# Sums of the exponentials in window attention: one product of 294 columns over both halves of a unit in place of two of 147

## The chip, the cores and the metric

The kernel runs on one core of a Trainium2 chip. The core has five engines that run side by side: TensorE (PE, with its weight loads shown apart as PEld), VectorE (DVE), ScalarE (ACT), GpSimd (POOL) and SyncE (SP, which here only starts transfers). The metric is the time of one execution on the device in microseconds (us); smaller is better. Everything is computed in 32-bit floating point.

## The reference

The input is 16 images of 56 x 56 tokens with 384 channels. Layer 0 normalizes each image over 32 groups of channels, rolls it, cuts it into 7 x 7 windows and runs attention with 12 heads of 32 channels inside each window, with a relative position bias and, at two borders, a mask. Layer 1 normalizes again and applies a 3 x 3 depthwise convolution with binary weights. Both are added to their input.

```
qkv = x @ w_qkv.T
score = einsum('bhwqd,bhwkd->bhwqk', q, k) / sqrt(32) + rel      # per window: 49 x 49
attn = softmax(score)                                            # exp, divided by its sum over the keys
out = einsum('bhwqk,bhwkd->bhwqd', attn, v) @ w_out.T + b_out
x = x + roll(out)
x = x + depthwise3x3(group_norm(x), sign(w))
```

The change concerns the sum over the keys in the softmax.

## The kernel before, in words

**Strips and units.** An image is cut into eight strips of seven rows (`NS` = 8), a strip has eight windows and is worked on in two units of four windows each (`UPS` = 2, `UW` = 4). There are 256 units in all; the even unit is the first of its strip, the odd one the second. In a strip of 392 tokens all large products have 392 columns: `query_key` (L472, tiles pq), `value` (L485, pv) and `project` (L656, py), each with three blocks of 128 input channels for each of its output tiles.

**The order.** Nothing is scheduled by a program at run time: `all_units` writes the instructions in the order in which every engine then takes them. `heavy(u)` lists the large products of a unit in six steps. An even unit has `value` of the next strip in steps 0 to 2 and half of `query_key` of the next strip in steps 3 to 5; an odd unit has the other half of `query_key` in steps 0 to 2 and `project` of its own strip in steps 3 to 5. After step 0 come, for the unit itself, `add_up`, `invert`, `attend` and `divide`. The `scores` and the `softmax` of the next unit follow step 2 in an even unit and step 3 in an odd one (`then`), and its `exponential` one step later. The normalization and the convolution of the image before lie between, as a list of due times (`plan_load`, `plan_conv`); the convolution's taps (L784) are DVE's largest work.

**A unit's attention.** A unit has two halves `r` of two windows `w` each. `scores` (L526) multiplies keys by queries with the array cut into tiles of 32 rows by 64 columns and puts the scores into the tile ps: four banks, one for each head `i` of a group of four, with the three groups `j` and the two halves `r` side by side (294 columns). The keys of window `w` lie on partitions 64w to 64w+48. `softmax` (L543) scales, adds the bias and writes the tile e in SBUF in the order (i, j, r, query); `exponential` (L561, ACT) replaces it by its exponential. `add_up` (L597) then sums over the keys with a matrix of ones: the array is cut into tiles of 64 rows by 32 columns, so eight tiles (four `i`, two `w`) can work side by side. Each product in 32 bits is two passes, and each pass is a weight load and a matmul instruction. The sums go into the columns 294 to 440 of ps's four banks, bank 2r+w. `attend` (L617) multiplies e by v, 48 products of 49 columns, into the two banks po, in the order j, r, i, w. The values v (two buffers) were put in place by `by_key` (L508), 16 transfers issued by SP during the even unit before; the first products of `attend` in an even unit wait for them.

**What follows the sums.** `invert` takes the logarithm (L635) and its negative exponential (L636) on ACT, and one step of refinement on DVE (L637, L638). The tiles ln and inv have 588 columns for each partition. L637 is the last to read ps, which has one buffer, so the `scores` of the next unit wait for it. `attend`'s result is copied out of po by ACT (L627), and `divide` (L645, DVE) multiplies it by the inverted sums; `project` waits for that.

**Banks.** Four further PSUM banks serve pq, pv, py and po in turn. So pv's second tile in an even unit takes the bank of the last py of the strip before, which DVE reads in L664 (the addition of y).

Of the kernel before, what the change touches and what calls it, by code (L numbers as in the profile page):

```python
# [9 lines left out]
F32 = mybir.dt.float32  # L10
I32 = mybir.dt.int32
AF = mybir.ActivationFunctionType
ALU = mybir.AluOpType
# [21 lines left out]
def kernel(  # L35
# [12 lines left out]
    nc = tc.nc  # L48
    P = 128
    B, H, W, C = x.shape  # L50
    NH = rel_table.shape[1]
    D = C // NH
    NC = C // P
    HPC = P // D
    T = WIN * WIN
# [3 lines left out]
    UW = 4  # L59
    UPS = NW // UW  # L60
    NU = NS * UPS
    HT = 64
# [21 lines left out]
    ptpool = ctx.enter_context(tc.tile_pool(name="pt", bufs=3))  # L84
# [14 lines left out]
    ones = const.tile([P, P], F32, tag="ones", name="ones")  # L99
# [20 lines left out]
    es = const.tile([P, NH, 2, HT], F32, tag="e", name="e")  # L120
# [334 lines left out]
    vs, ots, pts, ys = {}, {}, {}, {}  # L455
    raw, sums = {}, {}
# [127 lines left out]
    def by_head(u):  # L584

        flat = es.rearrange("k h w q -> k (h w q)")[:, : NH * 2 * T]
        return flat.rearrange("k (h r q) -> k h r q", h=NH, r=2)

    def add_up(u):

        e = by_head(u)
        su = raw[u][:, :, NC * 2 * T : NC * 3 * T]
        for r in range(2):
            for i in range(HPC):
                for w in range(2):
                    keys = slice(w * HT, w * HT + T)
                    nc.tensor.matmul(  # L597
                        su[i * D : (i + 1) * D, 2 * r + w].rearrange("p (j q) -> p j q", j=NC),
                        ones[keys, :D],
                        e[keys, i * NC : (i + 1) * NC, r],  # L600
                        start=True,
                        stop=True,
                    )
        sums[u] = su

    def attend(u, fast):
# [24 lines left out]
    def invert(u):  # L631

        su = sums[u]
        ln, inv = (ptpool.tile([P, UW, NC * T], F32, tag="pt", name=f"{name}_{u}") for name in ("ln", "inv"))
        nc.scalar.activation(ln, su, AF.Ln, bias=least)  # L635
        nc.scalar.activation(inv, ln, AF.Exp, scale=-1.0, accum_out=reach[:, 1, u : u + 1])  # L636
        nc.vector.scalar_tensor_tensor(ln, su, -1.0, inv, ALU.mult, ALU.mult)  # L637
        nc.vector.scalar_tensor_tensor(ln, ln, 2.0, inv, ALU.add, ALU.mult)  # L638
        sums[u] = ln

    def divide(u):

        s, n = divmod(u, UPS)
        ot = ots[s][:, :, n * UW * T : (n + 1) * UW * T].rearrange("p j (w q) -> p j w q", w=UW)
        nc.vector.tensor_tensor(ot, ot, sums.pop(u).rearrange("p w (j q) -> p j w q", j=NC), ALU.mult)  # L645

    def project(s, m):

# [322 lines left out]
    def all_units(fast):  # L971
# [13 lines left out]
        for u in range(B * NU):  # L985
            todo = heavy(u)
            light = [(w, f, a) for w, f, a in sorted(side.pop(u, []), key=lambda i: i[0])]
            more = u + 1 < B * NU

            then = NC if u % UPS else NC - 1  # L990
            for i in range(len(todo)):
                run(todo[i])
                if i == 0:
                    if fast:
                        add_up(u)
                    else:
                        for j in range(NC):
                            transpose(u, j)
                    if fast:
                        invert(u)  # L1000
                    attend(u, fast)
                    if fast:
                        divide(u)
                if i == then and more:
                    scores(u + 1, fast)
                    softmax(u + 1, fast)
                if i == then + 1 and more:
                    exponential(u + 1, fast)
                while light and light[0][0] - u <= (i + 1) / len(todo):
                    _, g, a = light.pop(0)  # L1010
                    g(*a)
            for _, g, a in light:
                g(*a)
# [112 lines left out]
```

## Time and profile before

| what | value |
|---|---|
| median of three runs | 4131.12 us (4129.32 to 4135.01) |
| span of the profiled execution | 4128.7 us |
| granted TensorE clock, mean | 0.991 |
| DVE: taps L784, 752 instructions | 1378.4 us busy, 1833 ns each |
| DVE: L637, L638, L645, 256 each | 765, 771, 771 ns each |
| ACT: L635, L636, L561, 256 each | 752, 693, 1185 ns each |
| PE: products of 392 columns, L472, L485, L656 | 1587.5, 814.5 and 816.1 us busy |
| PE: scores L526, 24576 instructions | 340.7 us busy, 225 ns each |

The span is that of the one execution that the profiler recorded, from its first to its last instruction; the median is of separate runs and is 2.4 us longer. "Busy" of PE is the union of the intervals in which at least one matmul ran; matmuls overlap, and their ends are modelled, so a group's busy time is smaller than its count times its mean. "Idle before" is the time that an engine stood still just ahead of the group, with what ended it. A timeline merges neighbours of one group; its columns are start, length, engine, line, operation, tiles, shape and count.

### The profile page before, as it was taken

Reading aid. Unit: us, or ns where it says so; the run is one execution under the profiler, and the core shown is the slowest. Engines: PE = TensorE matmul, PEld = TensorE weight load, DVE = VectorE, ACT = ScalarE, POOL = GpSimd, SP = SyncE. Lnnn points to the kernel's source line nnn. Section 1 sums busy time; section 2 is a strip of 40 time slices with the busy share of each in tenths; the row PEclk is TensorE's granted clock in tenths of the full one; section 3 lists DMA queues with packets and bytes.
Section 4 is the critical chain, followed back from the end, with each engine's and each line's share of the span. In section 5 each row is a group of like instructions: output and inputs, shape, how many; then the busy total and the mean of one; then the engine's idle time right before and its main releaser. Section 6 shows DMA issues by size and latency. Waiting matters only on the chain.

```text
span 4128.7 us, 153178 instructions
## 1 busy us (share of the span) xinstructions
PE 4041.2 (98%) x67257; PEld 2554.0 (62%) x67257; DVE 3495.7 (85%) x3711; ACT 2237.9 (54%) x4654; POOL 1875.3 (45%) x3165
## 2 busy tenths in 40 slices
PE   5999999999999999999999999999999999999997
PEld 3666666666666666666666666666666666666656
DVE  4555989889898998989889898988989889898897
ACT  2545646555565655655555564655556555564552
POOL 5444435545453554445445453554545455452000
PEclk8999999999999999999999999999999999999998
DMA  4434556555665665556555555665556565554544
GB/s 94 79 60 90 110 100 126 105 109 103 116 114 108 116 113 103 110 98 127 106 115 108 109 116 103 117 115 100 114 100 121 104 122 109 101 121 77 107 100 109
DMA packets 1524022, 439.45 MB, mean 106 GB/s; under 512 B 1458970, under 2 KB 1473979, under 8 KB 1523346
## 3 DMA queue, kind: packets, MB, share of 16 engines
q1 hardware_dynamic: 1432680, 267.66, 38.1%
q0 software_dynamic: 87648, 159.12, 15.7%
q8 instruction: 531, 8.70, 0.9%
q10 hardware_dynamic: 3018, 2.78, 0.3%
q14 instruction: 145, 1.19, 0.1%
HBM read 169.63 MB, written 158.46 MB: 79 GB/s over the span
## 4 chain that ended last, share of the span: by engine, by line
PE 68%; issue 10%; DVE 9%; POOL 7%; DMA 4%; ACT 1%; SPq 1%; DVEq 0%; ACTq 0%; POOLq 0%
PE pq L472 28%; PE pv L485 14%; PE py L656 13%; PE ps L526 6%; PE po L617 5%; POOL xl L419 5%; DVE o L784 4%; PE ps L597 3%; DMA xl<-in_x_dram 1%; DMA mvd<-mv 1%; DVE e L543 1%; SPq L508 1%; POOL dev L268 1%; DVE st L452 1%; DVE y L664 1%
## 5 line engine op out<-in xcount | busy, mean ns | idle before, releaser
L472 PE MATMUL pq<-xn,wq_t 128*128 128x392 f32 x4608 | 1587.5, 497 | 0.1
L419 POOL DMA_DIRECT2D xl<-in_x_dram x1980 | 1331.2, 722 | 162.1 <-DVE xt L436 99.6
L784 DVE SCALAR_TENSOR_TENSOR o<-hp,dw_t,o 128x1568 f32<-128x1568 f32 x752 | 1378.4, 1833 | 5.4
L472 PEld LDWEIGHTS pq<-xn,wq_t 128*128 128x128 f32 x4608 | 846.6, 188 | 596.5 <-issue 1.9
L485 PE MATMUL pv<-xn,wq_t 128*128 128x392 f32 x2304 | 814.5, 497 | 4.7 <-DVE y L664 3.5
L656 PE MATMUL py<-ot,wo_t 128*128 128x392 f32 x2304 | 816.1, 499 | 3.0 <-DVE ot L645 3.0
L479 ACT COPY qk<-pq 128x392 f32<-128x392 f32 x768 | 369.9, 483 | 661.1 <-PE pq L472 660.1
L676 POOL COPY y<-y 128x63 f32<-128x63 f32 x128 | 54.5, 426 | 1314.6 <-DVE y L664 1314.6
L656 PEld LDWEIGHTS py<-ot,wo_t 128*128 128x128 f32 x2304 | 427.4, 190 | 298.0 <-DVE ot L645 6.9
L485 PEld LDWEIGHTS pv<-xn,wq_t 128*128 128x128 f32 x2304 | 423.6, 188 | 304.1 <-DVE y L664 5.3
L561 ACT ACTIVATE e<-e 128x1176 f32<-128x1176 f32 x256 | 303.2, 1185 | 417.9 <-DVE e L543 416.9
L637 DVE SCALAR_TENSOR_TENSOR ln<-ps,inv 128x588 f32<-128x588 f32 x256 | 195.9, 765 | 386.0 <-ACT inv L636 381.2
L492 ACT COPY vt<-pv 128x392 f32<-128x392 f32 x384 | 189.3, 493 | 431.6 <-PE pv L485 430.9
L526 PEld LDWEIGHTS ps<-qk 32*64 32x64 f32 x24576 | 308.5, 131 | 144.3 <-issue 123.0
L617 PE MATMUL po<-e,v 49*32 49x49 f32 x24576 | 368.9, 212 | 8.8 <-DMA v<-vq 7.9
L617 PEld LDWEIGHTS po<-e,v 49*32 49x32 f32 x24576 | 357.9, 105 | 16.4 <-issue 8.8
L543 DVE SCALAR_TENSOR_TENSOR e<-ps,bias 128x1176 f32<-128x1176 f32 x256 | 347.3, 1357 | 14.2 <-PE ps L526 13.9
L526 PE MATMUL ps<-qk 32*64 32x49 f32 x24576 | 340.7, 225 | 1.7 <-DVE ln L637 1.6
L448 ACT COPY x<-xt 128x196 f32<-128x196 f32 x720 | 225.6, 368 | 173.8 <-DVE xt L436 173.6
L496 DVE STREAM_TRANSPOSE vq<-vt 128x512 f32<-128x512 f32 x384 | 265.8, 693 | 8.9 <-ACT vt L492 5.4
L664 DVE TENSOR_TENSOR y<-py,x 128x392 f32<-128x392 f32 x384 | 213.2, 555 | 51.2 <-PE py L656 47.9
L461 ACT ACTIVATE xn<-x,coef 128x392 f32<-128x392 f32 x384 | 247.1, 711 | 14.5 <-DMA coef<-cod 14.5
(173 smaller groups left out, 3349.6 us busy)
## 6 DMA issues: line engine op xcount, KB each, us to landing
v<-vq SPq DMA_DIRECT2D x2048, 48.0 KB
xb<-mid SPq DMA_DIRECT2D x90, 855.5 KB
out_dram<-o SPq DMA_DIRECT2D x736, 98.0 KB
mid<-y POOLq DMA_DIRECT2D x112, 619.5 KB
xl<-in_x_dram POOLq DMA_DIRECT2D x1260, 52.5 KB
mid<-y POOLq DMA_DIRECT2D x15, 354.0 KB
xl<-in_x_dram POOLq DMA_DIRECT2D x180, 28.0 KB
mid<-y POOLq DMA_DIRECT2D x15, 265.5 KB
```

The lines of the kernel that those rows point to most:

```text
L419: nc.gpsimd.dma_start(xz[i * D + lo : i * D + hi, c, k : k + n, :], flat[token : token + n * (hi - lo)].rearrange("(k t) c -> t k c", k=n) ...
L472: nc.tensor.matmul(pq[:, :ST].rearrange("p (w t) -> p w t", t=T), wq_t[:, c, m * P : (m + 1) * P], xn[:, c, :, :T], start=(c == 0), stop=( ...
L479: nc.scalar.copy(qk[:, m, :ST], pq[:, :ST])
L485: nc.tensor.matmul(pv[:, :ST].rearrange("p (w t) -> p w t", t=T), wq_t[:, c, 2 * C + m * P : 2 * C + (m + 1) * P], xn[:, c, :, :T], start= ...
L496: nc.vector.transpose(vq[:, :, :, m].rearrange("p h n d -> p n h d"), vt[:, m].rearrange("p (n w) (j b) -> p n (w j) b", w=2, b=D),)
L526: nc.tensor.matmul(pp[row * HT : (row + 1) * HT, i, k0 : k0 + T], qk[part, NC * fast + j, q0 : q0 + HT], qk[part, NC * (not fast) + j, q0 ...
L543: nc.vector.scalar_tensor_tensor(e, pp[:, :, : NC * 2 * T].rearrange("q i (n k) -> q i n k", k=T), QSCALE, bias[:, int(s % NS == NS - 1)]. ...
L561: nc.scalar.activation(flat, flat, AF.Exp, accum_out=reach[:, 0, u : u + 1])
L617: nc.tensor.matmul(po[w][i * D : (i + 1) * D, (2 * j + r) * T : (2 * j + r + 1) * T], vs[s][keys, n * 2 + r, h * D : (h + 1) * D], by_head ...
L656: nc.tensor.matmul(py[:, :ST], wo_t[:, c, m * P : (m + 1) * P], ots[s][:, c, :], start=(c == 0), stop=(c == NC - 1),)
L664: nc.vector.tensor_tensor(view.rearrange("p r (w c) -> p w r c", c=WIN), py[:, :ST].rearrange("p (w r c) -> p w r c", r=WIN, c=WIN), xs[s] ...
L784: nc.vector.scalar_tensor_tensor(acc, by_half(hp[:, dy : dy + BR, dx : dx + W]), dw_t[:, c, t : t + 1], acc, ALU.mult, ALU.add)
```

## The change

`add_up` gives the array both halves `r` at once. In the tile e the three groups `j` and the two halves `r` of a head `i` are contiguous, 3 x 2 x 49 = 294 elements, so one product for each `i` and `w` has 294 columns where there were two, one for each `r`, of 147. The result goes into the first 294 columns of the first two banks of ps, where the scores of heads `i` = 0 and 1 were, and no longer beside the scores of all four banks. The tiles ln and inv keep their 588 columns, now as 2 x 294, and `divide` reads them in the new order. All else is unchanged.

```diff
     def add_up(u):
 
-        e = by_head(u)
-        su = raw[u][:, :, NC * 2 * T : NC * 3 * T]
-        for r in range(2):
-            for i in range(HPC):
-                for w in range(2):
-                    keys = slice(w * HT, w * HT + T)
-                    nc.tensor.matmul(
-                        su[i * D : (i + 1) * D, 2 * r + w].rearrange("p (j q) -> p j q", j=NC),
-                        ones[keys, :D],
-                        e[keys, i * NC : (i + 1) * NC, r],
-                        start=True,
-                        stop=True,
-                    )
+        flat = es.rearrange("k h w q -> k (h w q)")[:, : NH * 2 * T]
+        su = raw[u][:, 0:2, : NC * 2 * T]
+        for i in range(HPC):
+            for w in range(2):
+                keys = slice(w * HT, w * HT + T)
+                nc.tensor.matmul(
+                    su[i * D : (i + 1) * D, w],
+                    ones[keys, :D],
+                    flat[keys, i * NC * 2 * T : (i + 1) * NC * 2 * T],
+                    start=True,
+                    stop=True,
+                )
         sums[u] = su
...
     def invert(u):
 
         su = sums[u]
-        ln, inv = (ptpool.tile([P, UW, NC * T], F32, tag="pt", name=f"{name}_{u}") for name in ("ln", "inv"))
+        ln, inv = (ptpool.tile([P, 2, NC * 2 * T], F32, tag="pt", name=f"{name}_{u}") for name in ("ln", "inv"))
...
     def divide(u):
 
         s, n = divmod(u, UPS)
-        ot = ots[s][:, :, n * UW * T : (n + 1) * UW * T].rearrange("p j (w q) -> p j w q", w=UW)
-        nc.vector.tensor_tensor(ot, ot, sums.pop(u).rearrange("p w (j q) -> p j w q", j=NC), ALU.mult)
+        ot = ots[s][:, :, n * UW * T : (n + 1) * UW * T].rearrange("p j (r w q) -> p j r w q", r=2, w=2)
+        nc.vector.tensor_tensor(ot, ot, sums.pop(u).rearrange("p w (j r q) -> p j r w q", j=NC, r=2), ALU.mult)
```

## The prediction

> **What bounds the kernel now.** I read the page's busy shares first, then the groups by line, then the timeline of PE over two strips, then the instructions of the two lines concerned in one unit of each kind.
>
> ```profile
> PE 4041.2 (98%) x67257; PEld 2554.0 (62%) x67257; DVE 3495.7 (85%) x3711; ACT 2237.9 (54%) x4654; POOL 1875.3 (45%) x3165
> ...
> L617 PE MATMUL po<-e,v 49*32 49x49 f32 x24576 | 368.9, 212 | 8.8 <-DMA v<-vq 7.9
> ...
> L597 PE MATMUL ps<-e,ones 49*32 49x147 f32 x8192 | 188.8, 291 | 6.6 <-ACT e L561 6.5
> ```
>
> PE is busy in 98% of the span, and in 3886 of the 3896 us from 124 to 4020 us (the view by windows). So an interval removed from PE's stream is time, unless another engine is late behind it. The changed line has 188.8 us; its neighbour L617, which follows it in every unit, 368.9 us.
>
> ```profile
> 1993.22 0.74 PE L597 MATMUL ps<-e,ones 49*32 49x147 f32 x32
> 1993.75 1.23 PE L617 MATMUL po<-e,v 49*32 49x49 f32 x96
> ...
> 2008.39 0.73 PE L597 MATMUL ps<-e,ones 49*32 49x147 f32 x32
> 2008.93 1.66 PE L617 MATMUL po<-e,v 49*32 49x49 f32 x96
> ...
> 2024.01 0.73 PE L597 MATMUL ps<-e,ones 49*32 49x147 f32 x32
> 2024.54 1.28 PE L617 MATMUL po<-e,v 49*32 49x49 f32 x96
> ...
> 2039.24 0.73 PE L597 MATMUL ps<-e,ones 49*32 49x147 f32 x32
> 2039.77 1.27 PE L617 MATMUL po<-e,v 49*32 49x49 f32 x96
> ```
>
> The columns are start, length, engine, line. The same 96 instructions of `attend` take 1.66 us in the unit at 2008 and 1.23 to 1.28 us in others. Over the whole trace they take 1.284 us on average in the odd units (the second of a strip) and 1.594 us in the even ones, the first unit left out. What differs is seen in the instructions of L617 inside the long one:
>
> ```profile
> L617 PEld LDWEIGHTS po<-e,v x15: 102/103/105, 2008.8 to 2009.6; 49*32 49x32 f32 x15
> L617 PE MATMUL po<-e,v x14: 200/201/202, 2008.9 to 2009.5; 49*32 49x49 f32 x14
> L617 PEldq EVENT_SEMAPHORE  x6: 51/51/51, 2008.9 to 2009.5; - x6
> ...
> L617 PEldq EVENT_SEMAPHORE  x2: 51/51/51, 2008.5 to 2008.6; - x2
> ```
>
> Between 2008.8 and 2009.6 only 14 of 96 products start, between event-semaphore instructions; two more of these stand earlier, during the sums. There are 949 of them on L617 in the trace: eight in most even units (they wait for the sixteen DMAs of `by_key`, landed long before), five in the units of the kind at 2039.77, none in odd ones.
>
> **What the Trainium skill says.** "TensorE: Matmul & The Clock Gate", the table at its head: TensorE's queue is 64 instructions deep, a partial reorder window that pulls weight loads ahead of running matmuls. The trace agrees. The 32 products of one unit's sums are, with their loads, 64 instructions. In an odd unit (starts in ns after the first sum) the sums start in four waves of eight, at 0-47, 153-200, 278-326 and 404-453. The loads of `attend` start at 406, 466, 483, 500 and so on to 583, then nothing to 720. The first sum ends at 310, its second pass at 153+283=435, the second pass of the first product of the second half at 404+283=687; the stops end 31 to 33 ns after the last two (466, 720). So an instruction enters as one leaves, in program order. "Perfetto Trace Analysis", Identifying Dependency Chains: a wait on several engines may get event-semaphore instructions put ahead. They are the 949 above; in the trace an event semaphore and the waiting load behind it repeat every 125 ns. "PSUM — Partial Sum Buffer", The four PSUM rules: one output fits one bank, 512 fp32 columns; 294 do. No run here shows that limit.
>
> **The change part by part.** Built, the two programs have the same instructions and waits in the same order on all five engines, but for the sums: 16 products of 147 columns become 8 of 294, each issued as two passes, so 32 load and product pairs become 16. The wait of the first one (for the exponential) stays.
>
> (a) The streaming. Waves of 147 columns are 126 ns apart, products of 392 columns 329 ns: 0.829 ns a column and 4 ns each, so 248 ns for 294. The second wave starts 27 ns late today (153 instead of 126); kept, the new ones start at 0 and 126+27-126+248=275, and `attend` can start at 523 against 531 now. 8 ns by 256 units is 2.0 us. Nearly all columns stream as before, so this is all that the product itself gives.
>
> (b) The room in the queue. With 32 instructions for the sums instead of 64, 32 of `attend` (16 pairs, the first half of its first `j`) can enter before the first sum starts, and all its event semaphores stand among those 16 pairs. They need 8 by 125 ns, 1.0 us. It is there: the exponential that the sequencer passes first ends 2.7 us (median) before an even unit's sums, at the least 0.98 us in the full stretch, and the last pv products (329 ns a pass) run meanwhile. In the even units the chain of waits, now from 460 to 1161 ns after the first sum, should be gone, and `attend` takes what it takes in an odd unit. Price: 1.594-1.284=0.310 us by 127 units=39.4 us. The five-semaphore units (1.27 us) already have no loss and are in the mean.
>
> (c) Odd units gain nothing more: the queue holds 16 pairs of `attend` when it stops at 583 now; after, 16 or 17 when it stops until the second pass of the first sum ends, 275+406+33=714 against 720.
>
> (d) Who is late next. Where pv waits for the addition of y, an earlier end of `attend` is only a longer wait:
>
> ```profile
> PE pv L485 <- DVE y L664: 3.5, 13, 0.4
> ...
> PEld pv L485 <- DVE y L664: 5.3, 13, 0.6
> ```
>
> This is one even unit of an image's eight, 15 of 127 (13 named here); their 0.35 us each are lost: -5.3 us. In the other even units pv comes 0.6 us or more after the addition, so 0.37 us less leaves it uncovered nowhere. The next scores come 1.1 us or more after L637 has read the sums. L656 after L645 stands in odd units, whose timing stays. DVE is the fullest: 29.88 of 30.80 us in one strip's window, 0.9 us left for 0.37. Cover is thin there; I take no loss and keep 10 us of it for the range.
>
> (e) Reading the sums. L635 and L637 read two banks by 294 instead of four by 147: 588 elements either way (752 and 765 ns), at nothing. L645 reads them in runs of 49 as before; heads and halves merge into one step, so it stays a three-step pattern. 771 ns; at most 0.15 us more, beside other PE work. The read scores are used up before the exponential, so writing on them adds no wait.
>
> Sum: -39.4+5.3-2.0=-36.1 us. The span 4128.7 gives 4092.6; the median of the runs, 4131.1, is 2.4 us above the profiled span, so 4095. I take 4096, with a microsecond for DVE.
>
> **The rivals.** The uncertainty of this measurement is about 0.2%, 8.3 us; I call less no change.
>
> A, only the streaming: the sequencer doesn't pass `attend`'s waits while sums stand unfinished, so they come when they come now. For it: the first two stand at 111-141 and 236-266 ns in the even units, never before the sums. Against: by then the queue is full, which explains it too, and in the scores a load that waits (the 30th or so) goes through with the first burst. It gives 4131-2=4129; up to 4125.
>
> B, DVE takes the place: the fullest strips (four of eight) give back what they gain, 12 to 25 us, because taps delay the division and the additions. For it: the 0.9 us above, and py after L645 by 0.1 us in one odd unit of eight. Against: DVE still waits 0.2 to 2 us for L636 in most units. It gives 4108 to 4120, say 4113.
>
> C, slower: the queue's room isn't counted in instructions but is tied to the sums as a group, so that `attend` enters only as sums leave. Longer passes leave later: the first pair at 310+123+33=466 instead of 343, the next at 714 instead of 466. Every unit would then lose 0.25 us, 63 us in all: 4194. An eighth of it is past the bound. It decides if fewer than two pairs of `attend` enter before the first sum ends. For it: no `attend` load starts before 406 now. Against: 33 pairs get in before the first stop both for sums (147 columns) and for scores (49 columns), so it counts instructions.
>
> D, that the change doesn't do what it says: the built order shows that it does.
>
> **How the numbers follow.** Forecast 0.70, own range 4084 to 4108: below by the odd units' best (1.18 us instead of 1.28, 12 us), above by the DVE term. B 0.11, A 0.09, C and any other loss 0.10. The range that leaves out no more than 0.2 reaches from 4082 to 4124: it takes in B and the edge of A. Faster by over 0.2% is the forecast and B, 0.81; within, A, 0.09; slower 0.10.
>
> **What would show it.** L597 with 4096 products of 294 columns, about 405 ns each and 186 us busy: (a). L617's busy time near 256 by 1.28, that is 328 to 335 us with the union of overlaps, from 368.9; even units at 1.2 to 1.3 us; its event semaphores before the sums' start: (b). Odd units within 0.03 us of now: (c). More waiting of pv for L664 in that one unit of eight, and no new waits of PE on DVE: (d). L635, L637 and L645 at 752, 765 and 771 ns: (e). Event semaphores still between the products of `attend` would make it A; odd units at 1.5 us, C.

## The result, and the profile after

The changed kernel takes 4110.36 us (median of four runs, 4108.16 to 4112.23); the kernel before, run beside it, 4131.23 us (4129.32 to 4135.01). The ratio is 0.9949, with an interval from 0.9935 to 0.9963: 20.9 us faster, where 35 were forecast. The profiled execution has a span of 4108.1 us at a clock of 0.991, as before.

The page of the changed kernel (all lines behind the edit have moved up by one, so L617 is now L616):

```profile
span 4108.1 us, 144986 instructions
...
PE 4017.7 (98%) x63161; PEld 2490.6 (61%) x63161; DVE 3496.3 (85%) x3711; ACT 2236.7 (54%) x4654; POOL 1873.2 (46%) x3165
...
L616 PE MATMUL po<-e,v 49*32 49x49 f32 x24576 | 345.5, 212 | 10.3 <-DMA v<-vq 9.6
```

PE has 4096 products fewer and is busy 23.5 us less (4041.2 before); nearly all of it is `attend`, 345.5 us after 368.9. DVE's busy time is the same. The groups by line show the sums and what reads them:

```profile
L636 DVE SCALAR_TENSOR_TENSOR ln<-ps,inv 128x588 f32<-128x588 f32 x256 | 196.1, 766 | 368.5 <-ACT inv L635 367.9 <-PE po L616 0.4
...
L596 PE MATMUL ps<-e,ones 49*32 49x294 f32 x4096 | 186.3, 421 | 6.5 <-ACT e L561 6.4
```

The sums lost 2.5 us of busy time (188.8 before). Their readers cost what they did (766 ns here; 753 for L634 and 771 for L644). The timeline of PE over an even and an odd unit:

```profile
1999.23 0.73 PE L596 MATMUL ps<-e,ones 49*32 49x294 f32 x16
1999.75 1.45 PE L616 MATMUL po<-e,v 49*32 49x49 f32 x96
...
2014.62 0.73 PE L596 MATMUL ps<-e,ones 49*32 49x294 f32 x16
2015.14 1.29 PE L616 MATMUL po<-e,v 49*32 49x49 f32 x96
```

The unit at 1999 is one with eight event semaphores. Its `attend` takes 1.45 us where such units took 1.66, but the forecast was 1.2 to 1.3. An event semaphore is here an instruction of its own, ahead of a load that has several semaphores to wait for; in this trace the load names one of them and the event semaphore the rest. The instructions of L616 in the 0.92 us from the first sum on (count, shortest, median and longest duration in ns, first and last start):

```profile
L616 PEld LDWEIGHTS po<-e,v x14: 103/104/107, 1999.5 to 2000.1; 49*32 49x32 f32 x14
L616 PE MATMUL po<-e,v x13: 200/203/203, 1999.8 to 2000.1; 49*32 49x49 f32 x13
L616 PEldq EVENT_SEMAPHORE  x8: 51/51/51, 1999.3 to 2000.1; - x8
```

All eight are still there, and none stands before the first sum: the same line has no instruction from 1995 to 1999.23. That is the prediction's step (b), which had put all eight ahead of the sums, seen to fail in one row.

Over all units, from the first sum to the first large product behind `attend`, which is the stretch that the change can reach (ns, means of 127 units of each kind, read from the starts in the trace):

| | before | after | difference |
|---|---|---|---|
| even units | 2102 | 1976 | -126, 16.0 us in all |
| odd units | 1743 | 1702 | -41, 5.2 us in all |
| `attend` alone, even / odd | 1594 / 1284 | 1450 / 1256 | -144 / -28 |
| first event semaphore after the first sum, median | 105 | 21 | -84 |

The two differences make 21.2 us: the whole gain lies here, and what was lost and won elsewhere cancels. The mean of the even units hides a spread. Their median falls by 185 ns (from 2105 to 1920), but the units where pv waits for y gain nothing, and in a few others v landed later than before.

Where the gain comes from shows in one even unit, the same in both traces (ns after its first sum). Before, the event semaphores of `attend` start at 141 and 266; then comes a stop until 460, and then one starts every 125 ns to 1085, with the last waiting load at 1161. After, they start at 21, 146, 271 and so on every 125 ns to 896, with no stop, and the last waiting load at 972. The chain of waits is the same, but it begins 120 ns earlier in this unit (84 at the median) and has no stop at the full queue, 69 ns more: 189 ns less at its end. Forecast was that all of it would lie before the first sum.

What the chain costs can be read inside the changed kernel's trace, since not all even units have eight event semaphores. The median stretch is 1591 ns in the 16 units with five, 1650 in the 13 with six and 1930 in the 96 with eight (1730, 1845 and 2117 before). So from six to eight each one adds about 140 ns (136 before), and five cost less than their number would make them: they lie in part behind the sums.

### The profile page after: what moved, and what is told of

Read it like the earlier page. It is cut to its first block, busy times and chain, and to the rows that moved or that the text cites. A ratio compares the mean times of both kernels' runs of the same rounds, so it can differ in the third digit from the quotient of the medians.

```text
span 4108.1 us, 144986 instructions
## 1 busy us (share of the span) xinstructions
PE 4017.7 (98%) x63161; PEld 2490.6 (61%) x63161; DVE 3496.3 (85%) x3711; ACT 2236.7 (54%) x4654; POOL 1873.2 (46%) x3165
## 4 chain that ended last, share of the span: by engine, by line
PE 50%; issue 18%; POOL 13%; DVE 8%; DMA 7%; SPq 2%; ACT 1%; DVEq 0%; ACTq 0%; POOLq 0%
PE pq L472 21%; PE pv L485 10%; PE py L655 9%; POOL xl L419 8%; PE ps L526 4%; DVE o L783 4%; PE po L616 3%; DMA mvd<-mv 2%; PE ps L596 2%; POOL dev L268 2%; DMA xl<-in_x_dram 1%; DMA gt<-mvd 1%; SPq L508 1%; DMA mid<-y 1%; DVE e L543 1%
## 5 line engine op out<-in xcount | busy, mean ns | idle before, releaser
L485 PE MATMUL pv<-xn,wq_t 128*128 128x392 f32 x2304 | 815.9, 497 | 8.1 <-DVE y L663 7.0
L485 PEld LDWEIGHTS pv<-xn,wq_t 128*128 128x128 f32 x2304 | 424.2, 188 | 308.2 <-DVE y L663 8.7
L655 PEld LDWEIGHTS py<-ot,wo_t 128*128 128x128 f32 x2304 | 426.4, 190 | 300.1 <-DVE ot L644 10.5
L616 PEld LDWEIGHTS po<-e,v 49*32 49x32 f32 x24576 | 352.2, 105 | 55.5 <-issue 11.4
L616 PE MATMUL po<-e,v 49*32 49x49 f32 x24576 | 345.5, 212 | 10.3 <-DMA v<-vq 9.6
L496 DVE STREAM_TRANSPOSE vq<-vt 128x512 f32<-128x512 f32 x384 | 266.0, 694 | 9.9 <-ACT vt L492 6.5
```

The lines of the kernel that those rows point to most:

```text
L485: nc.tensor.matmul(pv[:, :ST].rearrange("p (w t) -> p w t", t=T), wq_t[:, c, 2 * C + m * P : 2 * C + (m + 1) * P], xn[:, c, :, :T], start= ...
L496: nc.vector.transpose(vq[:, :, :, m].rearrange("p h n d -> p n h d"), vt[:, m].rearrange("p (n w) (j b) -> p n (w j) b", w=2, b=D),)
L616: nc.tensor.matmul(po[w][i * D : (i + 1) * D, (2 * j + r) * T : (2 * j + r + 1) * T], vs[s][keys, n * 2 + r, h * D : (h + 1) * D], by_head ...
L655: nc.tensor.matmul(py[:, :ST], wo_t[:, c, m * P : (m + 1) * P], ots[s][:, c, :], start=(c == 0), stop=(c == NC - 1),)
```

## The experiments

Twelve kernels ran, each against the kernel before in interleaved runs (4131 to 4133 us in all of them). Two questions were put to them: is it the queue's room that made the gain, and why did the event semaphores not move ahead of the sums?

### Layout or queue: two products again, in the new place

`split_outer` keeps the changed kernel's banks, readers and layout and gives each sum in two products of 147 again, all first parts first.

```diff
-        for i in range(HPC):
-            for w in range(2):
-                keys = slice(w * HT, w * HT + T)
+        for at in (0, NC * T):
+            for i in range(HPC):
+                for w in range(2):
+                    keys = slice(w * HT, w * HT + T)
...
-                    su[i * D : (i + 1) * D, w],
+                        su[i * D : (i + 1) * D, w, at : at + NC * T],
```

> The kernel after, but each sum product of 294 columns is issued as two of 147 into the same two banks, all first parts before all second parts: the layout of the change without its smaller count of instructions (32 weight load and product pairs a unit again). Queue theory (the gain is the room for attend's instructions and waits behind fewer sums): all of the gain is gone, 4131 us, within 6 of the kernel before; the event semaphores of attend stand again from about 100 ns after the first sum and the last of them past 1.1 us. Rival (the gain is in the layout, the banks or the reading of the sums): 4110 us, as after.

Measured 4131.34 us, ratio 0.9999 (0.999 to 1.0007): all of the gain is gone, even units at 2100 ns and odd ones at 1749. `attend` is back where it was (368.9 before):

```profile
L617 PE MATMUL po<-e,v 49*32 49x49 f32 x24576 | 370.0, 212 | 8.8 <-DMA v<-vq 8.2
```

New banks, two in place of four, and the new order of ln and inv are worth nothing that these runs can tell.

`split_inner` has the same products, with the two parts of one sum next to each other.

```diff
+                for at in range(0, NC * 2 * T, NC * T):
...
-                    su[i * D : (i + 1) * D, w],
+                        su[i * D : (i + 1) * D, w, at : at + NC * T],
```

> As split_outer, with the two parts of 147 columns one after the other for each tile of the array instead of all first parts first. Same count, same columns, same banks, another order. Queue theory with leaving in program order: the four passes of the first tile must end (about 690 ns) before the second tile's entries leave, so only four pairs of attend are in by 720 ns instead of sixteen; even units lose 0.26 us, odd ones 0.10 us, about 40 us in all: 4160 to 4175 us. Rival (the queue doesn't matter, only columns and banks do): equal to split_outer.

Measured 4168.85 us, ratio 1.0093 (1.0078 to 1.0109), as forecast. Its groups by line:

```profile
L617 PE MATMUL po<-e,v 49*32 49x49 f32 x24576 | 406.4, 212 | 8.3 <-DMA v<-vq 7.7
...
L597 PE MATMUL ps<-e,ones 49*32 49x147 f32 x8192 | 200.3, 291 | 6.4 <-ACT e L561 6.2
```

The loss is again in `attend` (406.4 us), though nothing of it was touched, and this time in odd units too (1902 ns). In one of them `attend` starts its second load at 465 ns, its third at 529, its fourth at 591 and its fifth at 716; in `split_outer` seven have started by 533. The first product of `attend` starts 528 to 530 ns after the first sum in both kernels, so it is the loads behind it that come in more slowly. With this pair it is shown that the number and the order of the products ahead of `attend` make the difference, and not the layout. That they act through a queue which empties in program order is the explanation that forecast both times.

### Taking the waits out of attend by a copy

If event semaphores are what is left, then `attend` without waits for transfers should be faster still. `after_own` lets ACT copy v, once its transfers have landed, into a second tile that `attend` reads; `before_own` does so in the kernel before. Both leave v and its copy one buffer each where v had two (not in the lines shown).

```diff
+    def own(s):
+        vs[s] = vpool.tile([P, NW // 2, C], F32, tag="vv", name=f"vv_{s}")
+        nc.scalar.copy(vs[s], vk.pop(s))
...
+                if i == then and more and u % UPS:
+                    own(u // UPS + 1)
```

> The kernel after, with one more step: the transfers of by_key land in a staging tile, and ACT copies it (1536 columns, about 1.5 us a strip) in the odd unit before, ahead of the exponential. attend then waits for no transfer and has no event semaphores. Theory (what the change left on the table is the chain of event semaphores that begins only 20 ns after the first sum): even units' attend becomes as long as odd ones', 0.19 us shorter in 127 units, of which the 16 that wait for the addition of y gain nothing: minus 21 us, 4089 us. Rival (even units are longer for another reason, or ACT's copy delays the exponential): 4110 us or more.

> The kernel before, with the same staging tile and ACT copy, so that attend has no event semaphores. Theory: even units' attend falls from 1.59 to 1.28 us, minus 34 us, 4097 us; and against after_own the change of the sums is then worth only what odd units gain, 0.04 us by 256, 8 to 10 us. Rival (the change's gain lies in the sums themselves): the two with the copy still differ by about 21 us.

Both forecasts missed by some 320 us: 4412.18 us (ratio 1.0668, 1.0653 to 1.0682) and 4418.98 (1.0688, 1.0673 to 1.0702). The waits of `after_own` say why (us in total, times, longest):

```profile
ACT vv L561 <- DMA v<-vq: 544.9, 99, 10.9
...
PE pv L485 <- ACT xn L461: 228.3, 75, 6.2
```

The copy came before its data: ACT stood 5.5 us at it in 99 of 128 strips, and behind it on ACT was xn, for which PE waited. The single buffers are not what held the transfers up: among the waits of SP for them none names the copy. Still the event semaphores of `attend` were gone, and the even units' stretch fell to a median of 1591 ns (1602 in `before_own`).

`after_late` and `before_late` put the copy behind the last large product of the odd unit.

```diff
-                if i == then and more and u % UPS:
+                if i == 2 * NC - 1 and more and u % UPS:
```

> The changed kernel, with v copied by ACT from the tile that the DMAs fill into a second one, as in after_own, but placed behind the last large product of the odd unit, behind the exponential. attend then waits for no DMA. Theory (the event semaphores of attend in the even units are what the change left over, because the sequencer reaches them only when the first sum has started): even units end like odd ones, 1.73 us from the first sum to the next large product where they take 1.98 now, 0.24 us by 127 units less about 4 us where pv waits for y: 4110-27=4083 us (4076 to 4096), and the copy, 1.47 us on ACT, delays nothing there because the transfers have landed by then. Rival (the copy on ACT itself, or single buffers of v, cost the 300 us of after_own, not the place where ACT waited): well above 4131.

> The same copy of v at the same place in the kernel before. Theory: even units go from 2.10 us to the odd ones' 1.77, 0.33 us by 127 units less 5 us where pv waits for y: 4131-37=4094 us (4086 to 4106). With no waits in attend the change itself is then worth only the odd units' part, 8 to 13 us (ratio of the two about 0.9975), not 21. Rival (the change's gain has nothing to do with the event semaphores): the two kernels stay 21 us apart.

Measured 4154.03 us (ratio 1.0049, 1.0035 to 1.0063) and 4159.31 (1.0063, 1.0049 to 1.0077): missed again, by 71 and 65 us. The waits of `after_late`:

```profile
ACT vv L561 <- DMA v<-vq: 100.0, 36, 10.5
...
PEld po L621 <- ACT vv L561: 97.8, 64, 11.8
```

In 36 strips v still lands after the copy's turn, and each even unit keeps one event semaphore. The median of the even units is 1593 ns, their mean 2129: most gained a third of a microsecond, and a few strips lost several.

### The waits met earlier on PE

Two kernels add an unused product of 12 columns to each even unit, in the tiling of the large products (128 by 128), into free columns of pv's bank. In `after_first` it stands behind the value products and reads e, so that it takes the wait for the exponential from the first sum:

```diff
+        if m == 0 and s - 1 in vs:
+            met = es.rearrange("k h w q -> k (h w q)")[:, :NH]
+            nc.tensor.matmul(pv[:, 512 - NH :], ones, met, start=False, stop=True, skip_group_check=True)
```

> The changed kernel, with an unused product of 12 columns of e behind the value products at the start of each even unit, in their tiling of the array (128 by 128). It takes the wait for the exponential, so the first sum of an even unit waits for nothing; only the change of the array's tiling stands between value and the sums. It costs an estimated 0.1 to 0.25 us in each of 127 even units, 13 to 32 us. Theory 1 (the sequencer does not pass a change of the tiling before the array has drained): attend's event semaphores still start about 20 ns after the first sum, the even units' attend keeps its length, time 4123 to 4142. Theory 2 (it was held by the first sum's wait for ACT): the event semaphores stand before the first sum, the even units' attend is as short as the odd ones', time 4096 to 4115.

Measured 4123.04 us, ratio 0.9977 (0.9968 to 0.9987), 13 us above the changed kernel: at the lower end of what theory 1 gave. The instructions of `attend` (L619 here) in the 0.92 us after the first sum of one even unit, at 2007.36:

```profile
L619 PEld LDWEIGHTS po<-e,v x14: 102/104/108, 2007.6 to 2008.2; 49*32 49x32 f32 x14
L619 PE MATMUL po<-e,v x13: 201/203/204, 2007.9 to 2008.2; 49*32 49x49 f32 x13
L619 PEldq EVENT_SEMAPHORE  x7: 51/51/51, 2007.4 to 2008.1; - x7
```

Nothing of the line stands before that sum, and over all even units the first event semaphore comes 20 to 23 ns after it, as in the changed kernel, though the sum now waits for nothing. So the wait for the exponential did not hold the sequencer, the part of PE that takes the instructions in program order. What is left between value and the sums is the change of the array's tiling.

`after_met` puts the product between the first and second value product and lets it read v, so that it takes all the waits for transfers:

```diff
+            if c == 0 and m == 0 and s - 1 in vs:
+                nc.tensor.matmul(
+                    pv[:, 512 - NH :], ones, vs[s - 1][:, 0, 0:C:D], start=False, stop=True, skip_group_check=True
+                )
```

> The changed kernel, with an unused product of 12 columns of v between the first and the second value product of each even unit, in their tiling (128 by 128). It takes all the waits for the DMAs of v ahead of the sums, on PE itself. It costs an estimated 13 to 32 us. Theory (event semaphores in a stream of large products are hidden in the run-ahead, those behind the change of tiling are not): they stand 1 us or more before the first sum, the even units' attend takes what the odd ones' takes, time 4083 plus 13 to 32 us: 4096 to 4115. Rival (event semaphores cost PE their time wherever they stand): at least 1 us more in each even unit, above 4200.

Measured 4189.48 us, ratio 1.0132 (1.0117 to 1.0148). The time was missed by some 80 us and the mechanism met. In the unit whose first sum starts at 2038.63, the instructions of the added line (L493):

```profile
L493 PEldq EVENT_SEMAPHORE  x4: 51/51/822, 2032.5 to 2033.6; - x4
L493 PEld LDWEIGHTS pv<-v,ones x2: 188/188/188, 2036.7 to 2037.0; 128*128 128x128 f32 x2
L493 PE MATMUL pv<-v,ones x2: 184/222/259, 2037.0 to 2037.0; 128*128 128x12 f32 x2
```

and those of `attend` in its first 0.92 us:

```profile
L620 PEld LDWEIGHTS po<-e,v x40: 102/106/108, 2038.9 to 2039.5; 49*32 49x32 f32 x40
L620 PE MATMUL po<-e,v x36: 200/203/226, 2039.1 to 2039.5; 49*32 49x49 f32 x36
```

One of them lasts 822 ns, a wait that is met while the products ahead run. Event semaphores in a stream of one tiling stand far ahead: 6.1 us before the first sum here, 3.1 us before the load they belong to (medians over all units: 5.8 us before the sum). `attend` then starts 36 products in the time in which it started 13. The stretches of all 256 units make 441.2 us in place of 484.1, 43 us less. Nine of these only moved: they are the wait for the first v, in the first unit. The loss is ahead of the sums. PE sat idle 62.9 us before the added product, in its waits mostly

```profile
PE pv L493 <- DMA v<-vq: 53.3, 25, 11.9
```

From the first value product to the first sum an even unit takes 2292 ns at the median, where it took 2068. Over all units that stretch is 111 us longer. Less the 43 this makes 68 of the 82 us by which the span grew; the rest was not followed up (the clock was 0.983).

### Is it the landing, then?

Since v lands late, two things can make even units long: the event semaphores, or the landing itself. `after_v16` lays v out so that each transfer moves runs of 1536 bytes in place of 128.

```diff
-                    v[half * D : (half + 1) * D].rearrange("k n (m c) -> k (n m) c", m=NC)[:, :, i * D : (i + 1) * D],
-                    vq[i * D : (i + 1) * D, half].rearrange("k n m d -> k (n m) d"),
+                    v[half * D : (half + 1) * D, i].rearrange("k n m d -> k (n m d)"),
+                    vq[i * D : (i + 1) * D, half].rearrange("k n m d -> k (n m d)"),
```

> The changed kernel with v laid out by head, window pair, block, so that each of the sixteen transfers of by_key moves runs of 1536 bytes in place of 128; the same sixteen transfers, waits and products. Theory: the packets of these transfers fall to a twelfth and they land sooner, but attend's sixteen event-semaphore waits stay where they are, behind the change of tiling. Only the 8 us in which PE waits for the landing itself may go: 4102 to 4111 us, even units at 1.95 to 1.98 us as now. Rival (the even units' extra time is the landing of v, not the event semaphores): even units come down to the odd ones' 1.73 us, about 4080.

Measured 4109.15 us, ratio 0.9939 (0.9926 to 0.9953): the changed kernel's time. Even units take 1962 ns. Longer runs gain nothing, and PE still waits 8.1 us for these transfers.

`after_v16_late` and `before_v16_late` join it with the late copy (both edits as shown above).

> after_late and after_v16 together: v copied by ACT behind the last large product of the odd unit, from transfers with runs of 1536 bytes. Theory (after_late lost its gain to transfers that land after the copy's turn, 100 us of waiting on ACT and 65 us on PE): the copy finds its data, PE's waiting for L561 falls below 10 us, and the event semaphores are gone, so the even units take 1.59 to 1.68 us as they do in after_met: 4110-43=4067 us, 4060 to 4085. Rival (the copy's 1.47 us on ACT is itself late for something): 4110 or more.

> The same two edits in the kernel before. Theory (all but a few us of the change's gain is the room it makes for event semaphores at the start of attend; without them the medians of after_own and before_own differ by 11 ns in the even units and 20 ns in the odd ones, 4 us in all): 2 to 8 us above after_v16_late, about 4072 us. Rival (the change gains by itself): 15 to 21 us above it.

Measured 4126.37 us (0.9983, 0.9977 to 0.999) and 4136.59 (1.0006, 0.9998 to 1.0014). The first forecast missed by 59 us, the second, of 4072 us, by 65. The waits of `after_v16_late`:

```profile
ACT vv L561 <- DMA v<-vq: 61.6, 26, 9.6
...
PE po L620 <- ACT vv L561: 43.1, 43, 10.3
```

The longer runs removed a third of the waiting and no more. The trace places the rest: v lands late in those strips because it is issued late. Where ACT stood waiting, the copy starts 2.2 us (median) after SP began to issue the last of the sixteen transfers; in the other strips it starts 5.1 us after. SP issues the first one 0.03 us after DVE has turned the last part of v (L496), and the last of the sixteen 13.6 us after the first, 10.5 in the other strips, with transfers of the output among them.

What the three pairs do give is the worth of the change once `attend` has at most one event semaphore a unit: 6.8 us (own), 5.3 us (late) and 10.2 us (late with long runs), where it is 20.9 us with them. The intervals of the first two pairs overlap, so only the last difference is clear of the noise. It is outside its forecast of 2 to 8 us, and well below the rival's 15 to 21. The stalls of the copy differ a little between the two sides, so these are not exact.

### Fewer event semaphores, nothing else moved

A wait for one semaphore needs no event semaphore. In the built program the 16 transfers of `by_key` take eight queues in turn, and one product of `attend` reads rows from two of them, four places apart, on two queues. `after_pair` issues the quarters of the keys in the order 0, 2, 1, 3. The two are then eight apart and share a queue: one wait.

```diff
-        for half in range(2 * part, 2 * part + 2):
+        for half in (part, 2 + part):
```

> The changed kernel with by_key's quarters issued in the order 0, 2, 1, 3 in place of 0, 1, 2, 3. The two transfers that one product of attend needs then stand eight apart, on the same queue, so in most even units six of its eight double waits become single ones, which need no event semaphore. No other instruction is added or moved. Theory (the event semaphores, 125 ns each with their load, set the start of attend in the even units): two of eight are left, the chain ends at about 0.4 us after the first sum instead of 0.97, hidden under the sums, and the even units come from 1.98 to about 1.7 us: 0.28 by some 110 units less 3 us where pv waits for y, 4110-28=4082 us (4074 to 4094). Rival (single waits on transfers cost the sequencer as much as double ones): 4106 to 4112.

Measured 4089.56 us (4086.33 to 4092.92), ratio 0.9897 (0.9881 to 0.9914): inside the forecast, 20.8 us below the changed kernel and 42.9 below the kernel before it was run against. The line of `attend` in its page, and its instructions in the 0.92 us from the first sum of an even unit, at 1985.48:

```profile
L616 PE MATMUL po<-e,v 49*32 49x49 f32 x24576 | 309.3, 213 | 15.4 <-DMA v<-vq 15.2
```

```profile
L616 PEld LDWEIGHTS po<-e,v x39: 102/106/108, 1985.8 to 1986.4; 49*32 49x32 f32 x39
L616 PE MATMUL po<-e,v x36: 201/203/226, 1986.0 to 1986.4; 49*32 49x49 f32 x36
L616 PEldq EVENT_SEMAPHORE  x2: 51/51/51, 1985.5 to 1985.6; - x2
```

The event semaphores of L616 fall from 949 to 365, and the even units' median from 1920 to 1591 ns (mean 1976 to 1801). Where two are left, as in 86 of 127 units, the second starts 146 ns after the first sum, and the six loads with a single wait behind them start 6 to 8 ns apart. The median is that of the kernels without any event semaphore there (1591 ns in `after_own`), and of the units with five in the changed kernel. So it is the event semaphores that cost the time, and no wait for data was taken away. The odd units came down too, by 38 ns, though the edit takes nothing from them; that 5 us is not explained. All stretches together gave 27 us, of which 6 were lost elsewhere. What the edit gives in the kernel before was not run.

## Why the prediction was right or wrong

**The direction and the bound: right; the range only in part.** PE sets the end, and an interval taken from its stream was time: the 21.2 us found in the stretches are the 20.9 us of the medians. The forecast's own range, 4084 to 4108 us, was missed by 2 us. The wider one, to 4124, holds the measured time because it took in rival B, whose mechanism did not happen: that part is luck.

**(a) The streaming: right.** The second wave starts at 272 ns (275 forecast) and `attend` at 519 (523). The products have 4096 instructions and 186.3 us busy, as foreseen, at a mean of 421 ns in place of 405.

**(b) The step that failed, the room for the waits:** "all its event semaphores stand among those 16 pairs. They need 8 by 125 ns, 1.0 us. It is there". The count of instructions was right: with 32 of the sums in the queue, the stop at 266 to 460 ns is gone. The time for the waits was not there. It was taken from the gap between the exponential and the sums, as if the sequencer could work through the sums and reach `attend` while pv still ran. It reaches the sums only when the array is about to start them: the first event semaphore stands 20 to 23 ns after the first sum in every even unit, with the wait for the exponential (`after`) and without it (`after_first`), while inside one tiling it stands 3 to 6 us ahead (`after_met`; and the 127 event semaphores of L485 stand 3.88 us, median, before their load in both kernels). Those run no further either: none of L485 starts more than 0.2 us before the first `project` product behind the scores, which is where their tiling begins. The Trainium skill, "TensorEngine Tiling (Array Packing)", Key Properties, says that switching the tiling mode drains TensorE. The traces agree so far that the first sum starts 420 ns after the last value product in the even units of both kernels, where value products are 329 ns apart; and they add that the run-ahead over waits ends there too. That the tiling alone does it is inferred: a kernel with sums in the tiling of value was not tried. The term was 39.4 us, 34.1 with the loss of (d), and came to 16.0; the even units' `attend` went from 1.594 to 1.450 us, not to 1.284. The price of the chain had been put too low, if anything. The odd units' length was taken for what is left without it, but without it, and without the waits for the landing, even units take 1695 ns on average in `after_met`, 407 less than before, where 310 was used. The units with five event semaphores were taken to have no loss, and they gained 0.14 us (median).

Rival A ("the sequencer doesn't pass `attend`'s waits while sums stand unfinished, so they come when they come now") was nearer, since none of the waits stands before the sums. But the sequencer does pass them while sums run: the first comes at 21 ns, and a sum takes 421. They come 84 ns earlier than before, with half as many instructions ahead of them, and the full queue no longer interrupts them. The sign against A that the prediction gave, that the queue was full and explained it too, held for the stop and not for the start: at 105 ns the queue had not yet been in the way.

**(c) Odd units: too low by 5 us.** Forecast at 714 against 720 ns for the resumption, and so no gain; the mean fell by 41 ns. The start of `attend` gives 12 of it. Another 22 are stops of 107 to 214 ns that fall inside `attend` in some units, often about 500 products apart: 97 ns per odd unit before and 75 after. What they are was not tested.

**(d) The addition of y: right in place.** The waits of the changed kernel:

```profile
PEld pv L485 <- DVE y L663: 8.7, 13, 0.8
...
PE pv L485 <- DVE y L663: 7.0, 13, 0.6
```

They have doubled on PE, from 3.5 us. That unit of each image gained nothing: its stretch went from 2391 to 2464 ns. No wait of PE on DVE came in elsewhere, so rival B (DVE takes the place, 4108 to 4120 us) gave the measured time by a mechanism that didn't happen.

**(e) The readers: right**, at 753, 766 and 771 ns. **Rival C** (4194 us) fell: in an odd unit eight loads of `attend` start between 274 and 320 ns, before the first sum has ended. What it feared is real in another order, though: `split_inner` lost 37 us.

Put together: the even units were to give 34.1 us by (b) and (d) and about 1 by (a), and gave 16.0; the odd ones were to give about 1, and gave 5.2. The term that was mis-sized is (b).

## What to carry to other kernels

Before counting on a queue's depth to hide waits, look in the trace at where the event semaphores of the line in question stand. In this kernel they ran microseconds ahead only where products of the same tiling stood between, and behind a change of tiling they started with its first product, where the sums covered about five of the eight. Here it paid more to make an instruction's waits single than to have them early: two transfers that one product needs together, put on one queue by the order of issue, gave 20.8 us. And a copy or an early wait that takes waits away from one place moves them to another with work queued behind it; the kernels with a copy were 16 to 302 us slower than the changed kernel, as the copy had to wait for late transfers.

## What the runs showed of the hardware

- On PE an event semaphore with the waiting load behind it took 125 ns, about 76 from the one to the load and 49 to the next (the changed kernel); loads with a single wait, met already, started 6 to 8 ns apart (`after_pair`).
- With 64 instructions of the sums ahead, the first event semaphore stood 105 ns after the first sum, with 32 ahead 21 ns. From the two, an estimate of 2.6 ns for each instruction.
- With the two products for the same tile of the array one right behind the other, the kernel took 37 us longer than with the same products in the other order (`split_inner` 4168.85 us, `split_outer` 4131.34).
- Two transfers of v issued eight apart share a semaphore, and a product that needs both has one wait in place of two: 365 event semaphores in place of 949 (`after_pair`).
- Runs of 1536 bytes in place of 128 in 2048 transfers of v changed nothing in the kernel's time (4109.15 against 4110.36 us).
